# An attention and mixture-of-experts block: heads in the inner loop, chunks of queries in the outer one

## The chip, the cores and the metric

The kernel runs on one core of a Trainium2 chip. The core has five engines that work side by side, each through its own list of instructions in order: PE (TensorE, matrix products; its weight loads are listed as PEld), DVE (VectorE), ACT (ScalarE), POOL (GpSimd) and SP (SyncE), which here only issues transfers. The metric is the time of one execution on the device in microseconds. All data are float32.

## The reference

There are 2048 tokens of 256 numbers. The block computes causal attention with 16 heads of 16 numbers, adds it to the input and normalises; then a mixture of experts, adds that and normalises again.

```
q = x @ Wq;  c = x @ Wkv_down;  k = c @ Wk_up;  v = c @ Wv_up      # c has 64 columns
q, k: rotary position on 12 of each head's 16 numbers
x1 = layernorm(x + softmax(mask(q @ k.T / 4)) @ v)
p = softmax(x1 @ gate.T)                      # 16 experts, the two best of each token
y = sum over the two: p_e * (silu(x1 @ w1_e.T) * (x1 @ w3_e.T)) @ w2_e.T    # 176 inner
z = the same form with one shared expert of 352 inner
out = layernorm(x1 + y + z)
```

## The kernel before

**Tiles.** The tokens are cut into four chunks c of 512 (CH), the heads into four groups g of four (G). The four heads of a group lie on 32 partitions each[...]. `prologue(c)` transposes a chunk of x into `xT[c]` and multiplies it down to `ckv[c]`. `project_k(g, c)` makes the rotated keys of a group and a chunk: two products on PE, two DVE instructions into the one buffer `rot` (pool wk1), and a POOL addition into `ks[g, c]`. `project_q` makes `qs[g, c]` (PE, then DVE), `project_v` makes `vs[g, c]` (PE, ACT, and a POOL fill of a column of ones). `double(g)` is three small POOL copies that complete a group's weights once they are loaded.

**Two passes of products.** A softmax needs the largest score of each query. The kernel first computes all scores for the maxima alone (`Maxima`, the tiles m: PE products, reduced on DVE into pm by `tensor_reduce`, or with the mask by `tensor_tensor_reduce` where keys and queries are of one chunk). When all maxima of (g, c) are there, `negated` gathers them into nm (DVE), and `shift` transposes nm on PE (pn) and adds it to the queries on DVE: the result is `qa[g, c]`. A second pass computes the scores transposed with qa (`Weighted`, tiles s), ACT takes exponentials (p), POOL masks the diagonal squares, and PE multiplies by the values (av). ACT copies av to `more` and POOL adds it to avs; in a step without m, DVE adds it directly. `finish(g, c)` transposes avs (po), divides by the sum and adds the result to x in `xr[c]`; after the last group it also takes means and variances.

**Steps.** The order is written out by hand in the list `steps`. Each step is a pair of an m unit (g, c, t, kc) and an s unit (g, c, kb), either of which may be missing. A unit is four products of up to 512 columns; it is "whole" where keys and queries are of different chunks, and "diagonal" where they are of one, with 512, 384, 256 and 128 columns in turn. In a pair the two halves interleave: two heads of s beside two of m, then the reverse. The av products of a step are issued after the products of the next step. The list before runs group by group: group 0 through chunks 0 to 3, then each other group from chunk 3 down to 0, and the last group through chunks 3, 0, 1, 2. `put(step, what)` hangs everything else on step numbers: projections, prologues, shift, finish, and the router. All eight PSUM banks are one rotating pool for these tiles (`bank`). PE keeps the order of the program; the other engines' lists are put in order when the kernel is built.

**Router and experts.** For a chunk with all groups finished, `normed` normalises on DVE, `turned` transposes to `x1T[c]`, `choose` computes logits (lg) and picks two experts, `settle` counts places (pc) and `scatter` sends each row by eight indirect transfers of POOL to its expert's room in the DRAM buffer xg, which SP filled with blank rows before. The chunk LAST is routed after attention. Then `table`, `load_block`, `turn`, `hidden`, `turn_hidden` and `output` run 47 blocks of 128 rows, each through the expert that its rows belong to, and POOL scatters the results to yg. `shared_hidden` and `shared_out` compute the shared expert; `fetch` and `combine` add up, normalise and write.

**Memory and loads.** Keys and values of the running groups live in the pool kv, eight buffers of k and six of v. The experts' weights w13 (44 KB on each partition) are loaded early by SP, after x, the rotary tables cs and cq and the projections' weights, and before the blank fill of xg. The rotary table for keys of chunk 3, cs3, has a tile of its own; the other three become the shared expert's weights later.

Of the kernel before, what the change touches and what calls it, by code (L numbers as in the profile page):

```python
# [17 lines left out]
P = 128  # L18
# [19 lines left out]
WARM = 3  # L38
LAST = 2
DEPTH = 6  # L40
# [6 lines left out]
def block_kernel(  # L47
# [39 lines left out]

    cs = [const.tile([P, 2, CH], F32, tag=f"cs{c}", name=f"cs{c}") for c in range(3)]

# [39 lines left out]
    for c in range(NCH):  # L129
        nc.gpsimd.tensor_copy(  # L130
            xr[c][:, :, E : E + 1], number[:, 4 * c : 4 * c + 4].unsqueeze(2)
        )

    blank = hot.rearrange("p j t n -> p (j t n)")[:, :ROW]
    nc.gpsimd.memset(blank, 0.0)
    nc.gpsimd.tensor_copy(blank[:, E : E + 1], number[:, TT:])

# [147 lines left out]
    with ExitStack() as att:  # L285
        ap1 = att.enter_context(tc.tile_pool(name="ap1", bufs=1))
        kv = att.enter_context(tc.tile_pool(name="kv", bufs=8))
        wk1 = att.enter_context(tc.tile_pool(name="wk1", bufs=1))
# [14 lines left out]
        )  # L303
        cs.append(ap1.tile([P, 2, CH], F32, tag="cs3", name="cs3"))
        cq = [ap1.tile([P, CH], F32, tag=f"cq{c}", name=f"cq{c}") for c in range(NCH)]
# [46 lines left out]
        load_rope(0, False, nc.sync)  # L352
        load_x(1)
        load_rope(0, True, nc.scalar)
        double(0)
        for a in range(2):
            nc.sync.dma_start(out=wvs[a * LAT : (a + 1) * LAT], in_=wv[:LAT])
        load_rope(1, False, nc.sync)
        load_rope(1, True, nc.sync)
        load_x(2)  # L360
        load_rope(2, False, nc.sync)
        load_rope(2, True, nc.sync)
        load_x(3)
        load_rope(3, False, nc.sync)
        load_rope(3, True, nc.sync)
        for g in range(1, G):
            load_weights(g, nc.sync)
        nc.sync.dma_start(out=gw, in_=gate.rearrange("(k p) n -> p k n", p=P))
        for j, w in ((0, w1), (1, w3)):
            for k in range(2):  # L370
                nc.sync.dma_start(
                    out=w13[:, k, :, j * INTER : (j + 1) * INTER],
                    in_=w[k * P : (k + 1) * P, :NF].rearrange("p (n f) -> p n f", f=INTER),
                )

        def load_shared():
# [4 lines left out]
            for i, (o, m) in enumerate(SCH):  # L381
                nc.sync.dma_start(out=sw2[:m, i, :], in_=w2[NF + o : NF + o + m, :])


        for e in range(NEXP):
# [28 lines left out]
        def project_k(g, c):  # L414
            tmp = wk1.tile([P, 2, CH], F32, tag="rot", name=f"rot{g}_{c}")
            pk = [bank(f"pk{g}_{c}_{a}") for a in range(2)]
            for a in range(2):
                r = slice(a * LAT, (a + 1) * LAT)
                matmul(
                    pk[a], lhsT=wks[g][r], rhs=ckv[c][r], start=True, stop=True  # L420
                )
            nc.vector.scalar_tensor_tensor(  # L422
                tmp[:, 0, :], pk[0], unit, cs[c][:, 0, :], ALU.add, ALU.mult
            )
            nc.vector.tensor_tensor(tmp[:, 1, :], pk[1], cs[c][:, 1, :], ALU.mult)  # L425
            ks[g, c] = kv.tile([P, CH], F32, tag="k", name=f"k{g}_{c}")
            nc.gpsimd.tensor_tensor(ks[g, c], tmp[:, 0, :], tmp[:, 1, :], ALU.add)  # L427
# [11 lines left out]
        def project_v(g, c):  # L439

            pv = [bank(f"pv{g}_{c}_{a}") for a in range(2)]
            for b in range(4):
# [6 lines left out]
                )  # L449
            v = kv.tile([P, CH], F32, tag="v", bufs=6, name=f"v{g}_{c}")  # L450
            for a in range(2):
# [47 lines left out]
        def shift(g, c, nm):  # L499

            pn = bank(f"pn{g}_{c}")
            for t in range(4):
                transpose(
                    pn[:, t * P : (t + 1) * P], nm[:, t].rearrange("p h d -> p (h d)"), ident
                )
            qa[g, c] = wk3.tile([P, CH], F32, tag="qa", name=f"qa{g}_{c}")
            nc.vector.tensor_tensor(qa[g, c], qs[g, c], pn, ALU.add)
# [83 lines left out]
        def diagonal_m(g, c):  # L591
            return [(g, c, t, c) for t in reversed(range(4))]
# [9 lines left out]

        def spread(whole, diagonal, n):

            out, whole = [], list(whole)
            for d in diagonal:
                out += whole[:n] + [d]
                whole = whole[n:]
            return out + whole

        def add(ms, ss, pattern=None):

            ms, ss = list(ms), list(ss)
            pattern = pattern or "1" * max(len(ms), len(ss))
            for p in pattern:
                steps.append((ms.pop(0) if ms else None, ss.pop(0) if p == "1" else None))
            assert not ms and not ss, (ms, ss)


        add(diagonal_m(0, 0), [], "0000")  # L620
        add(whole_m(0, 1), [], "0000")
        add(diagonal_m(0, 1), diagonal_s(0, 0))
        add(whole_m(0, 2), whole_s(0, 1, [0]), "00011011")
        add(diagonal_m(0, 2), diagonal_s(0, 1))
        add(whole_m(0, 3), whole_s(0, 2, [0, 1]), "000111101111")
        add(diagonal_m(0, 3), diagonal_s(0, 2))
        m = whole_m(1, 3)
        add(m[:4], [], "0000")
        add(
            spread(m[4:], diagonal_m(1, 3), 2) + diagonal_m(1, 2),  # L630
            spread(whole_s(0, 3, [0, 1, 2]), diagonal_s(0, 3), 2),
        )
        for g in range(1, G):
            add(
                spread(whole_m(g, 2), diagonal_m(g, 1), 2) + whole_m(g, 1),
                spread(whole_s(g, 3, [2, 1, 0]), diagonal_s(g, 3), 2),
            )
            if g + 1 == G:

                add(diagonal_m(g, 2), diagonal_s(g, 0))  # L640
                add([], diagonal_s(g, 1) + whole_s(g, 1, [0]))
                add([], whole_s(g, 2, [1, 0]) + diagonal_s(g, 2))
            else:
                m = whole_m(g + 1, 3)
                add(
                    spread(m[:8], diagonal_m(g, 0), 2),
                    spread(whole_s(g, 2, [1, 0]), diagonal_s(g, 2), 2),
                )
                add(
                    spread(m[8:], diagonal_m(g + 1, 3), 1),  # L650
                    spread(whole_s(g, 1, [0]), diagonal_s(g, 1), 1),
                )
                add(diagonal_m(g + 1, 0 if g + 2 == G else 2), diagonal_s(g, 0))

# [14 lines left out]

        for step, what, c in (  # L670
            (1, project_k, 1), (1, project_q, 1), (3, prologue, 2), (4, project_v, 0),
            (6, project_k, 2), (7, prologue, 3), (9, project_v, 1), (9, project_q, 2),
            (14, project_k, 3), (17, project_q, 3), (19, project_v, 2), (32, project_v, 3),
        ):
            if what is prologue:
                put(step, what, c)
            else:
                put(step, what, 0, c)
        for g in range(1, G):
            i = m_first[g, NCH - 1]  # L680
            put(5, double, g)
            for c in range(NCH):
                put(i + (-14, -11, -8, -6)[c], project_k, g, c)
                put(min(i + (32, 24, 13, -3)[c], m_first[g, c] - 3), project_q, g, c)
                put(i + (24, 22, 17, 13)[c], project_v, g, c)
        for (g, c), i in m_last.items():
            def late(i=i, g=g, c=c):
                nm = negated(g, c)
                put(i + 2, shift, g, c, nm)
            put(i, late)  # L690
            assert i + 3 <= s_first[g, c]
        for (g, c), i in s_last.items():
            put(i + (4 if g + 1 < G else 2), finish, g, c)
            if g == G - 1:
                put(i + 2, normed, c)
                if c != LAST:
                    put(i + 6, turned, c, bank)
                    put(i + 7, lambda c=c: chosen.update({c: choose(c, bank)}))
                    put(i + 11, lambda c=c: settle(c, bank, chosen[c]))
                    for t in range(4):  # L700
                        put(i + 12, scatter, c, t)

        put(s_first[G - 1, 3], load_shared)

# [4 lines left out]
        prologue(0)  # L709
        project_k(0, 0)  # L710
        project_q(0, 0)
        prologue(1)
        prior = None
# [258 lines left out]

    shared_hidden(3, 0)
    shared_hidden(3, 1)
    turned(LAST, spare)
    shared_hidden(3, 2)
    both = choose(LAST, spare)
    shared_out(3)
    shared_hidden(0, 0)
    settle(LAST, spare, both)  # L980
# [5 lines left out]
    key = keys(end)  # L986
    shared_hidden(0, 1)
    shared_hidden(0, 2)
    shared_out(0)
    shared_hidden(1, 0)  # L990
    turn(0)
# [10 lines left out]
    output(NBLK - 1, key)  # L1002
    shared_hidden(1, 1)
    shared_hidden(1, 2)
    shared_out(1)
    shared(LAST)
    fetched = {}
    for n, h in enumerate((6, 7, 0, 1, 2, 3, 4, 5)):
        fetched[h], load = fetch(h)
        if n == 0:  # L1010
            wait_for(back, load)
# [68 lines left out]
```

## Time and profile before

| | us |
|---|---|
| runs, median of three (lowest, highest) | 824.31 (823.65, 827.38) |
| the profiled execution, its own time | 821.03 |
| its span, first to last instruction | 819.3 |
| PE busy (share of the span) | 790.6 (96%) |
| DVE busy | 552.0 (67%) |
| ACT busy | 452.9 (55%) |
| POOL busy | 328.0 (40%) |
| first m product | 19.6 |
| last finish of attention begins | 597.65 |
| first product of an expert | 642.2 |

The span is what the profile's times count in; the execution's own time lies 1.7 us above it. The granted clock of PE is 0.988 of full speed on average. DMA moves 72.6 MB, most of it between 60 and 180 us, when the experts' weights and the blank rows go. A busy PE means only that a product is under way: products overlap, and their ends are modelled.

### The profile page before, as it was taken

Reading aid. Unit: us, or ns where it says so; the run is one execution under the profiler, and the core shown is the slowest. Engines: PE = TensorE matmul, PEld = TensorE weight load, DVE = VectorE, ACT = ScalarE, POOL = GpSimd, SP = SyncE. Lnnn points to the kernel's source line nnn. Section 1 sums busy time; section 2 is a strip of 40 time slices with the busy share of each in tenths; the row PEclk is TensorE's granted clock in tenths of the full one; section 3 lists DMA queues with packets and bytes.
Section 4 is the critical chain, followed back from the end, with each engine's and each line's share of the span. In section 5 each row is a group of like instructions: output and inputs, shape, how many; then the busy total and the mean of one; then the engine's idle time right before and its main releaser. Section 6 shows DMA issues by size and latency. Waiting matters only on the chain. (4 is left out here: it accounts for less than half of the span.)

```text
span 819.3 us, 15191 instructions
## 1 busy us (share of the span) xinstructions
PE 790.6 (96%) x5146; PEld 371.8 (45%) x5146; DVE 552.0 (67%) x1503; ACT 452.9 (55%) x1014; POOL 328.0 (40%) x562
## 2 busy tenths in 40 slices
PE   7999999999999999999999999999999899999994
PEld 3444433534333344534344444443356466666652
DVE  2769888986777887787887777887466233333266
ACT  1143556387776886676786668756531233333346
POOL 2042535344454554455354546433553133333300
PEclk9999999999999999999999999999899999999998
DMA  5479999960000000010000000001152322222062
GB/s 145 130 190 334 325 331 325 318 191 2 1 1 2 1 1 2 1 36 18 2 1 1 2 1 1 2 1 53 52 161 78 98 84 86 83 79 76 16 206 102
DMA packets 68339, 72.56 MB, mean 89 GB/s; under 512 B 5056, under 2 KB 62499, under 8 KB 68262
## 3 DMA queue, kind: packets, MB, share of 16 engines
q1 hardware_dynamic: 63006, 62.43, 26.3%
q0 software_dynamic: 3792, 8.43, 2.9%
q10 hardware_dynamic: 1464, 0.72, 0.4%
q8 instruction: 42, 0.69, 0.3%
q14 instruction: 35, 0.29, 0.1%
HBM read 27.10 MB, written 46.43 MB: 90 GB/s over the span
## 5 line engine op out<-in xcount | busy, mean ns | idle before, releaser
L534 ACT ACTIVATE p<-s 128x512 f32<-128x512 f32 (+3 forms) x640 | 292.7, 540 | 131.6 <-PE m L139 77.5
L139 PE MATMUL m<-k,q 32*128 32x512 f32 (+3 forms) x1280 | 303.3, 564 | 0.8 <-DVE rot L422 0.5
L139 PE MATMUL s<-qa,k 32*128 32x512 f32 (+3 forms) x1280 | 280.4, 558 | 3.3 <-DVE avs L562 2.3
L489 DVE TENSOR_REDUCE pm<-m 128x1 f32<-128x512 f32 x384 | 237.5, 681 | 44.0 <-PE m L139 43.6
L566 POOL TENSOR_TENSOR avs<-avs,more 128x512 f32<-128x512 f32 (+3 forms) x125 | 136.8, 1094 | 166.4 <-ACT more L565 162.8
L139 PEld LDWEIGHTS s<-qa,k 32*128 32x128 f32 x1280 | 107.3, 184 | 120.3 <-ACT p L534 67.4
L139 PE MATMUL av<-p,v 128*32 128x512 f32 (+3 forms) x1280 | 156.6, 546 | 0.9 <-ACT p L534 0.4
L139 PEld LDWEIGHTS m<-k,q 32*128 32x128 f32 x1280 | 122.8, 183 | 44.4 <-issue 12.0
L484 DVE CUSTOM_DVE_ANT_0 m<-m,qmask 128x512 f32<-128x512 f32 (+3 forms) x256 | 118.2, 521 | 28.8 <-PE m L139 25.8
L565 ACT COPY more<-av 128x512 f32<-128x512 f32 (+3 forms) x125 | 65.6, 525 | 38.3 <-PE av L139 31.4
L928 POOL DMA_INDIRECT yg<-yb,to x47 | 46.3, 985 | 99.1 <-DVE to L922 51.0
L538 POOL TENSOR_SCALAR_AFFINE_SELECT p<-p 128x128 f32<-128x128 f32 x256 | 70.6, 297 | 38.2 <-ACT p L534 36.4
L139 PEld LDWEIGHTS av<-p,v 128*32 128x32 f32 x1280 | 27.3, 108 | 104.5 <-ACT p L534 53.6
L139 PE MATMUL ph<-w,xbT 128*128 x188 | 68.8, 490 | 2.3 <-DVE xbT L881 1.7
L900 DVE TENSOR_TENSOR rh<-ru,ph 128x176 f32<-128x176 f32 x47 | 15.9, 337 | 61.9 <-ACT ru L898 61.9
L898 ACT ACTIVATE ru<-ph 128x176 f32<-128x176 f32 x47 | 14.9, 318 | 66.9 <-PE ph L139 65.6
L139 PE MATMUL py<-w2r,hT 88*128 x188 | 48.5, 380 | 0.5 <-ACT hT L907 0.5
L139 PE MATMUL h<-xT,cs 128*128 128x512 f32 (+1 forms) x96 | 43.3, 597 | 2.4 <-ACT u L791 1.4
L277 POOL DMA_INDIRECT xg<-xr,slot x32 | 31.1, 972 | 32.6 <-issue 21.3
L139 PEld LDWEIGHTS ph<-w,xbT 128*128 128x128 f32 x188 | 32.4, 191 | 23.2 <-issue 13.4
L139 PEld LDWEIGHTS py<-w2r,hT 88*128 88x128 f32 x188 | 35.5, 189 | 13.3 <-ACT hT L907 1.1
L427 POOL TENSOR_TENSOR k<-rot 128x512 f32<-128x512 f32 x16 | 20.3, 1268 | 42.6 <-DVE rot L425 42.6
(146 smaller groups left out, 649.0 us busy)
## 6 DMA issues: line engine op xcount, KB each, us to landing
xg<-hot SPq DMA_DIRECT2D x16, 2064.0 KB
xb<-xg SPq DMA_DIRECT2D x47, 129.0 KB
w<-in_w_dram SPq DMA_DIRECT2D x4, 1408.0 KB
got<-yg SPq DMA_DIRECT2D x8, 512.0 KB
w2r<-in_w_dram SPq DMA_DIRECT2D x2, 1408.0 KB
xr<-in_x_dram SPq DMA_DIRECT2D x4, 512.0 KB
out_dram<-o SPq DMA_DIRECT2D x8, 256.0 KB
cs<-in_rope_dram SPq DMA_DIRECT2D x16, 80.0 KB
```

The costliest lines, as they stand in the source:

```text
L139: tc.keep_in_program_order(op(*args, **kw))
L277: put = nc.gpsimd.indirect_dma_start(out=xg[:, :], out_offset=bass.IndirectOffsetOnAxis(ap=slot[:, j, i : i + 1], axis=0), in_=xr[c][:, t, ...
L427: nc.gpsimd.tensor_tensor(ks[g, c], tmp[:, 0, :], tmp[:, 1, :], ALU.add)
L484: nc.vector.tensor_tensor_reduce(out=ps[:, :n], in0=ps[:, :n], in1=qmask[:, CH - n :], scale=1.0, scalar=3.0 * NEG, op0=ALU.add, op1=ALU.m ...
L489: nc.vector.tensor_reduce(to, ps, AX.X, ALU.max)
L534: nc.scalar.activation(pr[:, n0:], ps[:, n0:], AF.Exp, scale=SCALE)
L538: nc.gpsimd.affine_select(out=diag, in_=diag, pattern=[[1, P]], base=0, channel_multiplier=-1, compare_op=ALU.is_ge, fill=0.0,)
L565: nc.scalar.copy(more[:, n0:], pv[:, n0:])
L566: nc.gpsimd.tensor_tensor(to, to, more[:, n0:], ALU.add)
L898: nc.scalar.activation(u, ph[:, :INTER], AF.Silu)
L900: nc.vector.tensor_tensor(us[b], u, ph[:, INTER:], ALU.mult)
L928: nc.gpsimd.indirect_dma_start(out=yg[:, :], out_offset=bass.IndirectOffsetOnAxis(ap=to[:, 0:1], axis=0), in_=yb, in_offset=None, bounds_c ...
```

## The change

The loops change places. Attention runs chunk by chunk, and all four groups within each chunk, from chunk 0 to chunk 3: job i is (g, c) with g running fastest. While job i's s units run, the whole m units of job i+1 and the diagonal ones of job i+2 run beside them; projections of k and q are made three jobs ahead. So keys and values of every group must stay to the end of attention: the pool kv goes, and the 32 tiles lie in `places`, 22 of them inside w13 and ten in tiles of their own. The weights of the experts are loaded in two halves by `load_experts` when groups 1 and 2 of the last chunk are done. All groups' projection weights are loaded at the start, three groups are projected before the first step, and the rotary tables of chunk 3 use the tile of chunk 0. Chunks 0, 1 and 2 are routed between the steps of the following chunk; LAST is 3. qa has two buffers instead of three, and the blank rows have a tile of their own. In the last stage chunks take each other's places.

```diff
-LAST = 2
+LAST = 3
...
-    cs = [const.tile([P, 2, CH], F32, tag=f"cs{c}", name=f"cs{c}") for c in range(3)]
+    cs = [const.tile([P, 2, CH], F32, tag=f"cs{c}", name=f"cs{c}") for c in range(NCH - 1)]
+    cs.append(cs[0])
...
-        kv = att.enter_context(tc.tile_pool(name="kv", bufs=8))
...
+        room13 = w13.rearrange("p k n f -> p (k n f)")
+        places = [room13[:, i * CH : (i + 1) * CH] for i in range(2 * NEXP * 2 * INTER // CH)]
+        places += [
+            ap1.tile([P, CH], F32, tag=f"kv{i}", name=f"kv{i}")
+            for i in range(2 * G * NCH - len(places))
+        ]
...
         load_weights(0, nc.scalar)
         load_rope(0, False, nc.sync)
-        load_x(1)
         load_rope(0, True, nc.scalar)
-        double(0)
+        load_weights(1, nc.sync)
+        load_weights(2, nc.sync)
         for a in range(2):
             nc.sync.dma_start(out=wvs[a * LAT : (a + 1) * LAT], in_=wv[:LAT])
+        load_weights(3, nc.sync)
+        for g in range(G):
+            double(g)
+        load_x(1)
         load_rope(1, False, nc.sync)
         load_rope(1, True, nc.sync)
         load_x(2)
+        load_x(3)
         load_rope(2, False, nc.sync)
         load_rope(2, True, nc.sync)
-        load_x(3)
-        load_rope(3, False, nc.sync)
         load_rope(3, True, nc.sync)
-        for g in range(1, G):
-            load_weights(g, nc.sync)
...
-            ks[g, c] = kv.tile([P, CH], F32, tag="k", name=f"k{g}_{c}")
+            ks[g, c] = places[2 * NCH * g + c]
...
-            v = kv.tile([P, CH], F32, tag="v", bufs=6, name=f"v{g}_{c}")
+            v = places[2 * NCH * g + NCH + c]
...
-            qa[g, c] = wk3.tile([P, CH], F32, tag="qa", name=f"qa{g}_{c}")
+            qa[g, c] = wk3.tile([P, CH], F32, tag="qa", bufs=2, name=f"qa{g}_{c}")
...
+        jobs = [(g, c) for c in range(NCH) for g in range(G)]
+        ahead = {0: (0, 0, 0, 0), 1: (2, 4, 4, 4), 2: (3, 6, 8, 8), 3: (4, 8, 12, 12)}
+        add(diagonal_m(*jobs[0]), [])
+        add(diagonal_m(*jobs[1]), [])
+        for i, (g, c) in enumerate(jobs):
+            ss = whole_s(g, c, reversed(range(c)))
+            ms = whole_m(*jobs[i + 1]) if i + 1 < len(jobs) else []
+            whole = [(ms[j], ss[j]) if j < len(ss) else (ms[j], None) for j in range(len(ms))]
+            whole = whole or [(None, u) for u in ss]
+            more = len(whole) - len(ss)
...
+            ds = diagonal_s(g, c)
+            dm = diagonal_m(*jobs[i + 2]) if i + 2 < len(jobs) else [None] * 4
+            diagonal = list(zip(dm, ds))
+            if c:
+                diagonal = diagonal[2:] + diagonal[1::-1]
...
+            if i + 3 < len(jobs):
+                put(d384, project_k, *jobs[i + 3])
+                put(d128, project_q, *jobs[i + 3])
+            if i + 1 < len(jobs):
+                put(d256, project_v, *jobs[i + 1])
+            if g == 0 and c + 1 < NCH:
+                put(d384, prologue, c + 1)
+        put(s_first[1, 0], load_rope, NCH - 1, False, nc.sync)
+        for k in range(2):
+            put(s_last[k + 1, NCH - 1], load_experts, k)
...
-                put(i + 2, shift, g, c, nm)
+                put(max(i + 2, s_first[g, c] - 3), shift, g, c, nm)
...
             if g == G - 1:
-                put(i + 2, normed, c)
-                if c != LAST:
-                    put(i + 6, turned, c, bank)
-                    put(i + 7, lambda c=c: chosen.update({c: choose(c, bank)}))
-                    put(i + 11, lambda c=c: settle(c, bank, chosen[c]))
+                put(i + (2 if last else 5), normed, c)
+                if not last:
+                    i += (40, 20, 8)[c]
+                    put(i, turned, c, bank)
+                    put(i + 2, lambda c=c: chosen.update({c: choose(c, bank)}))
+                    put(i + 6, lambda c=c: settle(c, bank, chosen[c]))
                     for t in range(4):
-                        put(i + 12, scatter, c, t)
+                        put(i + 8 + t, scatter, c, t)
...
         prologue(0)
-        project_k(0, 0)
-        project_q(0, 0)
-        prologue(1)
+        for n, job in enumerate(jobs[:3]):
+            project_k(*job)
+            project_q(*job)
+        project_v(*jobs[0])
```

The order that results, by step: 0 to 7 m alone (the diagonals of jobs 0 and 1), 8 to 27 chunk 0, 28 to 63 chunk 1, 64 to 115 chunk 2, 116 to 179 chunk 3. Steps 20, 22, 24, 25, 52, 54, 57, 60, 100, 102, 104 and 107 hold a whole m alone; 152, 157, 162 and 163 hold a diagonal s alone, and from 164 on all hold s alone.

## The prediction

> **What bounds the kernel now.** I read the stages first, as windows of busy time by engine: start, early attention, steady attention, the end of attention, the stretch up to the experts, the experts, the combination. Columns: busy time of PE, PEld, DVE, ACT, POOL (instructions), granted clock, DMA share, GB/s.
>
> ```profile
> 0.00:60.00 60.00, 53.54 (x254) 24.17 (x258) 34.04 (x97) 14.53 (x33) 15.46 (x56) 0.97 0.55 151
> 60.00:156.00 96.00, 95.83 (x652) 39.34 (x648) 81.49 (x176) 48.19 (x106) 39.29 (x68) 1.00 1.10 327
> 156.00:534.00 378.00, 376.35 (x3037) 158.07 (x3034) 298.64 (x743) 273.40 (x602) 183.76 (x320) 1.00 0.07 21
> 534.00:600.00 66.00, 62.08 (x430) 25.36 (x431) 44.58 (x180) 38.19 (x86) 28.39 (x57) 0.95 0.11 36
> 642.00:780.00 138.00, 136.63 (x564) 87.46 (x565) 43.69 (x138) 47.93 (x141) 45.71 (x47) 0.99 0.24 72
> ```
>
> The reader is to see that PE is busy everywhere, which says little: early attention holds 6.8 matmuls per us (652 in 96 us), steady attention 8.0. In the early stretch DVE is busy 85%, so PE stretches while it waits for banks; in the steady stretch DVE is busy 79%, ACT 72%, and PE's own pace counts. The pace is read from the timeline of one paired step (start, duration, engine, tile):
>
> ```profile
> 403.94 0.70 PE L139 MATMUL s<-qa,k 32*128 32x512 f32 x2
> 405.87 1.06 PE L139 MATMUL av<-p,v 128*32 128x512 f32 x8
> 406.86 0.70 PE L139 MATMUL s<-qa,k 32*128 32x512 f32 x2
> 408.02 2.07 ACT L534 ACTIVATE p<-s 128x512 f32<-128x512 f32 x4 [0.32 <-PE m L139]
> 408.10 2.48 DVE L489 TENSOR_REDUCE pm<-m 128x1 f32<-128x512 f32 x4 [0.22 <-PE m L139]
> ```
>
> From 403.94 to 405.87 run the eight products of m and s (1.93 us), then av (0.99): 2.92 us a step on PE, against 2.48 on DVE and 2.66 on ACT (2.07 and a 0.59 copy). A step with m alone is the reverse: PE 1.14, DVE 2.48. Last, the waits in 534 to 600 us (total us, times, longest):
>
> ```profile
> ACT p L534 <- PE s L139: 23.6, 17, 3.4
> DVE avs L562 <- PE av L139: 6.9, 7, 3.1
> DVE avs L562 <- PE s L139: 6.5, 2, 5.0
> ```
>
> No engine is full there: the routers of chunks 3, 0 and 1 lie between the last twenty steps, and PE, DVE and ACT wait for each other in turn.
>
> [...] The clock of 0.83 in 560 to 580 us fits: there products of s take 2.0 us for 1.1. [...] eight products of 32 rows take 1.93 us together, 0.59 to 0.70 each. A pair is thus as long as its longer half.
>
> **The method.** I price PE's program step by step and compare with the starts of steps in the trace (first product of s or m of each step). Prices from the timeline: paired 512 columns 1.93 + 0.99; 384: 1.67 + 0.78; 256: 1.46 + 0.57; 128: 1.25 + 0.37 (the four of a diagonal 9.02); m alone 1.14 (diagonal set 3.3); s alone 1.14 + 0.99 (diagonal set 6.0); project_k 1.13, project_q 1.98, project_v 1.15, shift and finish 0.6 each, a prologue 3.1, a router 3.9 (transposes 1.1, logits 1.94, counts 0.82). Before: 84 pairs with a whole s 245, 14 paired diagonal sets 126, m alone 21, s alone 37, projections with shifts and finishes 16 x 5.46 = 87, prologues 12, routers 12: 540 us. Attention ends at 598.3 (start of the last finish plus 0.6), so 58 us are lost, and by sections: before step 12 (59.7 us, 39.8 priced) 20; steps 12 to 49 (116.3 measured, 98.9 priced) 17, these hold twelve m-alone steps; steps 50 to 149 (327, 321) 6; step 150 to the end (93.9, 79) 15.
>
> **The change by parts.**
>
> *Products.* Both orders have 180 steps: 140 paired, 20 m alone, 20 s alone. Before, four diagonal m are paired with whole s and sixteen whole m are alone; after, eight diagonal and twelve whole are alone and all pairs match: 0.5 to 1 us less. Projections, routers, exponentials, reductions are as many as before. Priced: 539.5.
>
> *Start.* Three heads' groups are projected before the first m. SP issues weights 1 to 3 and wv before x1. The last sines of group 2 are issued at about 16.4 us (x0 and the rope loads end at 11.9 in the trace; 2 x 2.2 us of issues follow) and land some 2.5 later. By the built order POOL does the doublings of groups 1 and 2 ahead of the first k (end 19.8), and rot has one buffer, so k0 (1.27), rot1 (1.35), k1 (1.27), rot2 (1.35), q2 (0.7) run one after the other: DVE's first reduction starts at 25.8 instead of 20.78. Two diagonal sets on DVE (7.2 each and one shift) follow; PE runs two steps ahead through eight banks, so step 8 starts at 38.7. Priced work done by then is 20.8: 17.9 lost, and 2.5 in the first prologue behind exponentials. 20.4 against 20: +0.5. The later loads (x1 at 20, ropes to 44, the zero fill of xg 44 to 152 after 101 us of issues as now, the fourth rope behind it on SP) are due later still: the fourth rope at step 83, about 300 us. They cost nothing, covered by steps 8 to 83.
>
> *m alone.* Twelve whole ones, now laid between pairs in three jobs: DVE 20.3, 30.2, 40.2 us against PE 19.0, 30.7, 42.4. With the 7 to 10% that DVE-tight sections show now (12 to 24: 35.7 measured over 30.7): 10 lost for 17: -7.
>
> *Middle.* 116 other steps at the 0.06 us a step of steps 50 to 149 lose 7; two prologues wait for ACT, 1 us each; three routers put some 7 us of small DVE work each into stretches where DVE has 83 to 93% of PE's load: 4 in all; the dense first jobs 1.5. Together 14.5 against 6: +8.5. The scatters (24 x 1.27 us on POOL) hide under POOL's 50% idle time.
>
> *Borders of jobs.* Now shift precedes the first s by many steps. After, at eight borders (into chunk 1, chunk 2's first three, all of chunk 3) shift is issued after the job's last step and the next instruction on PE is s with that qa. Queued on PE: everything. The qa addition takes 0.68 and starts 0.07 after the transposes in the trace (404.07): 0.8 us each, 6.4, and 0.6 for DVE's backlog: +7. No trace shows this wait; its bounds are 0 (PE has av and a projection to do meanwhile) and 3.4 (DVE a whole step behind, 2.6 more).
>
> *End.* Twelve whole and four diagonal s alone with no router between: PE 2.13 a step, ACT 2.07. 2 lost for 15: -13. This includes the half clock (6.8 us at half, 3.4 lost).
>
> *Experts' weights.* 5.8 MB now go at about 507 and 552 us, behind nothing on SP; the zero fill moved at 320 to 345 GB/s, so 9 us for each half. Due at about 637: hidden by at least 75 us. K and V need no buffers to come free any more; none waited before. From the end of attention to the end the order is the same with chunks renamed: 221 us kept, in the experts' stage by 47 scatters on POOL and their landings.
>
> Sum: -0.5 + 0.5 - 7 + 8.5 + 7 - 13 = **-4.5 us**. The profiled execution took 821.03 (span 819.3), so it becomes 816.5; the median of the runs is 824.31, 3.3 above, so I predict **819.8**. A measurement of this kernel can tell about 0.5%, 4.1 us, from no change.
>
> **Rivals.**
> 1. *The borders decide: slower.* Without the borders the sum is -11.5 us, so from 1.4 us at each of the eight on the change loses. With DVE behind by 1.8 us, two thirds of a step's four reductions, each costs 2.6 and all 21: +9.5, 834. For it: DVE is at 93% of PE in the first job of chunk 3, and settle's work falls two steps before two borders. Against it: DVE drains while PE does av and projections.
> 2. *All bubbles go.* Borders covered by av and projections (-7), m alone costs only the greater of DVE and PE (-3): 809. For it: steps 50 to 149 lose 2% only, all extras included.
> 3. *No gain because the end is not freed:* the end's 15 us are lost again, as ACT waits for PE step by step (2.13 against 2.07), while the rest holds: 824 with some of the borders hidden. Against it: steps 167 and 171 took 2.07.
>
> **How the numbers follow.** Forecast 0.45, of it half beyond 4.1 us faster (0.24), 0.17 within, 0.04 slower; rival 2 0.22; rival 1 0.25; rival 3 0.08, nearly all within. Faster 0.46, same 0.24, slower 0.30. The likeliest case's own range is 813 to 827. Bounds: borders 0 to 24, m alone 3 to 17, routers and prologues 0 to 14, end 0 to 9, start -3 to +5; all together -20 and more to +26, and 806 to 836 leaves 2 in 10 out.
>
> **What would show it.** Right: first reduction near 26 us; step 8 near 39; last finish near 594; PE waiting for qa about eight times at 0.8 us; clock 1.00 in the last 40 us of attention; the stretch from there to the end within 1 us of 221. Wrong: a border above 1.4 us, early attention at under 7 matmuls per us in chunks 1 to 3, or a first product of an expert that waits for w13.

## The result, and the profile after

The changed kernel took **872.09 us** (median of four runs, 869.63 to 874.27) against 824.88 us for the kernel before (median of four, 823.65 to 827.38): 1.057 times as long, 95% interval 1.053 to 1.061. The profiled execution has a span of 871.8 us and a mean granted clock of PE of 0.952 (before: 819.3 and 0.988). Of these 52.5 us, 47.4 had been lost when the last step of attention began (595.2 us before, 642.6 now). The forecast was 819.8 us with a range of 806 to 836: it was wrong, in size and in sign.

The stages first. The first three windows are those of the prediction; the fourth reaches to the end of attention, which is later now, and the fifth holds the experts. Columns: busy time of PE, PEld, DVE, ACT and POOL with instructions, granted clock, DMA share, GB/s.

```profile
0.00:60.00 60.00, 53.93 (x262) 29.29 (x262) 34.62 (x121) 12.38 (x30) 19.11 (x62) 0.86 0.65 179
60.00:156.00 96.00, 91.09 (x660) 41.78 (x654) 72.65 (x218) 48.09 (x120) 40.74 (x95) 0.93 1.10 302
156.00:534.00 378.00, 360.09 (x2556) 149.60 (x2556) 286.37 (x723) 220.74 (x481) 170.31 (x273) 0.95 0.05 16
534.00:645.00 111.00, 108.64 (x889) 37.84 (x882) 69.36 (x130) 91.80 (x198) 37.88 (x70) 1.00 0.19 53
693.00:832.00 139.00, 137.47 (x563) 88.05 (x564) 42.87 (x138) 47.87 (x141) 45.31 (x47) 0.98 0.25 71
```

PE is still "busy" 95% of the third window, but it started 2556 products in the 378 us where the kernel before started 3037 (as the profile counts them: it has 24 records for the twelve products of a paired step), and its clock, which was 1.00 there, is 0.95. The loss is in the middle of attention. The end (fourth window) and the experts run at their pace.

A paired step that nothing disturbs costs what it did. Start, duration, engine, tile:

```profile
149.63 0.70 PE L136 MATMUL s<-qa,w 32*128 32x512 f32 x2
...
150.79 2.06 ACT L543 ACTIVATE p<-s 128x512 f32<-128x512 f32 x4 [2.19 <-PE m L136]
150.87 2.48 DVE L498 TENSOR_REDUCE pm<-m 128x1 f32<-128x512 f32 x4 [0.44 <-PE m L136]
...
151.56 1.06 PE L136 MATMUL av<-p,w 128*32 128x512 f32 x8
152.56 0.70 PE L136 MATMUL s<-qa,w 32*128 32x512 f32 x2
```

From 149.63 to 152.56 is 2.93 us, against the 2.92 of before. At the end of attention (534 to 645 us) ACT's waits for s, 23.6 us before, are down to 6.5:

```profile
ACT p L543 <- PE m L136: 10.3, 20, 2.1
ACT p L543 <- PE s L136: 6.5, 10, 1.6
...
DVE avs L571 <- PE av L136: 26.7, 16, 3.6
```

So the time went in single steps between. I priced each step as the prediction does and subtracted the price from the measured time. What is left is the loss, in us:

| steps | what lies there beside the pairs | lost |
|---|---|---|
| 28 to 35 | normalisation of chunk 0, a prologue | 10.0 |
| 64 to 75 | normalisation of chunk 1, choice and scatters of chunk 0, a prologue | 18.1 |
| 76 to 87 | choice of chunk 1 | 9.0 |
| 88 to 99 | scatters of chunk 1 | 7.5 |
| 116 to 131 | all of the router of chunk 2 | 19.0 |
| 20 to 27, 52 to 63, 100 to 115 | the m units alone | 13.3 |
| the other 71 between steps 12 and 179 | | 7.9 |

The first five rows are 64 us, and they hold the three routers. The waits of PE between 60 and 534 us say on which engines (total, times, longest):

```profile
PE s L136 <- DVE pm L498: 7.0, 6, 3.1
PE s L136 <- DVE qa L516: 4.9, 5, 1.2
PE av L136 <- issue: 3.4, 3, 1.7
PE av L136 <- POOL p L547: 3.1, 2, 2.4
```

The kernel before had next to none there; its longest was this:

```profile
PE s L139 <- DVE mv L585: 0.6, 1, 0.6
```

The four lines are 18 us only. In all PE was idle for 24.9 us between 60 us and the last s step, and for 4.5 us before. The rest is mostly the clock: between 100 and 500 us the trace has eight windows at half clock, 54.5 us together; the kernel before has none between 33 and 571 us. An estimate that counts half of their length as lost gives 27 us, where the one window of before, at 571 us, cost 3. So idle time (20 us more) and clock (24 more) make up 44 of the 47 us. Three of the windows, in the columns of above:

```profile
258.60:272.30 13.70, 13.70 (x54) 6.01 (x54) 9.05 (x29) 3.75 (x8) 1.50 (x2) 0.50 0.01 1
340.50:350.70 10.20, 9.78 (x26) 3.75 (x26) 4.63 (x16) 1.70 (x4) 1.88 (x5) 0.50 0.00 0
490.70:497.50 6.80, 6.20 (x22) 2.07 (x26) 3.62 (x6) 1.38 (x3) 0.82 (x1) 0.50 0.00 0
```

The timeline shows how it comes about. The first place is DVE at step 69, in the normalisation of chunk 1:

```profile
255.35 0.66 DVE L498 TENSOR_REDUCE pm<-m 128x1 f32<-128x512 f32 x1
255.93 0.16 DVE L151 TENSOR_SCALAR nv_ln<-mv 128x4 f32<-128x4 f32 x1
...
257.71 0.16 DVE L157 SCALAR_TENSOR_TENSOR na_ln<-nb_ln 128x4 f32<-128x4 f32 x1
257.79 0.68 DVE L498 TENSOR_REDUCE pm<-m 128x1 f32<-128x512 f32 x1
...
258.53 1.19 PE L136 MATMUL s<-qa,w 32*128 32x512 f32 x1 [0.48 <-DVE pm L498]
...
259.26 1.37 DVE L169 TENSOR_SCALAR xr<-xr,mv,nb_ln 128x256 f32<-128x256 f32 x4
...
260.55 2.47 DVE L498 TENSOR_REDUCE pm<-m 128x1 f32<-128x512 f32 x4
...
263.27 3.60 PE L136 MATMUL lg<-gw,xT 128*128 128x16 f32 x16
```

Between the reductions at 255.35 and 260.55 stand the dependent instructions of `inverse_root` and four of 0.34 us; only two of the reductions get between them. PE must wait for the banks that the reductions set free. No single wait is longer than 0.5 us, but few products start, and from 258.6 on each takes twice its time: lg 3.60 us for the 1.94 of the price list. The second place is POOL, at step 75:

```profile
292.89 0.97 POOL L274 DMA_INDIRECT xg<-xr,slot  x1 [0.31 <-ACT p L543]
293.88 0.30 POOL L547 TENSOR_SCALAR_AFFINE_SELECT p<-p 128x128 f32<-128x128 f32 x1
294.24 0.83 PE L136 MATMUL av<-p,w 128*32 128x384 f32 x2 [1.67 <-issue]
294.36 0.99 POOL L274 DMA_INDIRECT xg<-xr,slot  x1 [0.18 <-issue]
295.36 0.30 POOL L547 TENSOR_SCALAR_AFFINE_SELECT p<-p 128x128 f32<-128x128 f32 x1
295.72 1.11 PE L136 MATMUL av<-p,w 128*32 128x384 f32 x2 [0.65 <-POOL p L547]
...
296.77 3.35 PE L136 MATMUL pq<-xT,wqs 128*128 128x512 f32 x4
```

Each mask of a diagonal p stands behind a scatter, av waits for the mask, and pq then takes 3.35 us for 1.98.

### The profile page after: what moved, and what is told of

It reads as the page before. It is cut to its first block, busy times and chain, and to the rows that moved or that the text cites. A ratio compares the mean times of both kernels' runs of the same rounds, so it can differ in the third digit from the quotient of the medians.

```text
span 871.8 us, 15219 instructions
## 1 busy us (share of the span) xinstructions
PE 821.2 (94%) x5146; PEld 385.2 (44%) x5146; DVE 558.2 (64%) x1504; ACT 452.4 (52%) x1013; POOL 324.2 (37%) x561
## 5 line engine op out<-in xcount | busy, mean ns | idle before, releaser
L136 PE MATMUL s<-qa,w 32*128 32x512 f32 (+2 forms) x960 | 232.0, 574 | 14.1 <-DVE pm L498 7.0
L136 PE MATMUL m<-w,q 32*128 32x512 f32 (+3 forms) x960 | 236.2, 601 | 1.2 <-DVE rot L431 0.4
L575 POOL TENSOR_TENSOR avs<-avs,more 128x512 f32<-128x512 f32 (+3 forms) x124 | 133.3, 1075 | 210.0 <-ACT more L574 209.9
L136 PEld LDWEIGHTS s<-qa,w 32*128 32x128 f32 x960 | 89.2, 191 | 100.4 <-ACT p L543 55.2
L136 PEld LDWEIGHTS m<-w,q 32*128 32x128 f32 x960 | 98.4, 196 | 38.0 <-issue 9.9
L136 PE MATMUL av<-p,w 128*32 128x512 f32 (+3 forms) x864 | 110.0, 566 | 4.1 <-issue 3.4
L136 PE MATMUL m<-kv,q 32*128 32x512 f32 (+3 forms) x320 | 81.3, 574 | 2.1 <-DVE pm L493 1.4
L136 PE MATMUL s<-qa,kv 32*128 32x512 f32 (+3 forms) x320 | 63.9, 562 | 0.9 <-DVE qa L516 0.9
L136 PE MATMUL av<-p,kv 128*32 128x512 f32 (+3 forms) x416 | 53.6, 541 | 2.7 <-POOL p L547 2.7
L136 PEld LDWEIGHTS av<-p,w 128*32 128x32 f32 x864 | 17.8, 109 | 77.5 <-ACT p L543 37.7
L136 PEld LDWEIGHTS ph<-w,xbT 128*128 128x128 f32 x188 | 33.0, 195 | 23.9 <-issue 14.2
```

The costliest lines, as they stand in the source:

```text
L136: tc.keep_in_program_order(op(*args, **kw))
L575: nc.gpsimd.tensor_tensor(to, to, more[:, n0:], ALU.add)
```

## The experiments

The theories, by the names that the expectations use. **QUEUES**: a row of small DVE instructions or of scatters stands in order ahead of the reductions or the masks, PE waits for it, and its clock halves afterwards. **ORDER**: the loss belongs to the order chunk by chunk itself, to its borders, prologues and m units alone. **BUSY**: the routers cost their busy time, wherever they stand. **CLOCK**: the clock falls by itself. **HIDDEN**: idle time of DVE and POOL takes the work, as the prediction had it. Ratios are to the kernel before on the same chip, with 95% intervals; its median varied from 818.0 to 825.6 us over the chips that were used. Stages are compared by trace, and a trace too carries a difference between chips: the last s step of one and the same kernel (p3_both_pinned, p3_again) began at 598.7 us on one chip and at 601.4 on another.

### Four edits that the planner partly undid

The planner is the part of the build that puts the lists of DVE, ACT, POOL and SP in order.

**r1_routers_end** moves the routers in the program to the last job:

```diff
-                    i += (40, 20, 8)[c]
-                    put(i, turned, c, bank)
+                    i = s_first[jobs[-1]] + 4 * c
+                    put(i - 2, normed, c)
+                    put(i, turned, c, bank)
```

> The changed kernel with the routers of chunks 0, 1 and 2 (normalise, transpose, logits, choice, places, scatters) moved out of the middle of attention into the steps of the last job, 164 to 179, as the kernel before has them; the means and variances stay in the step of finish. QUEUES (the routers' small DVE instructions and their scatters on POOL stand in order ahead of the reductions and of the masks, PE waits for these, and its clock halves afterwards): steps 28 to 132 lose the routers' share, some 50 us, and the end gives 12 to 20 back: 825 to 840 us. ORDER (what was lost lies in the chunk-by-chunk order itself: waits for qa at every border, m units alone, prologues): 860 us or more, with long steps still at 33, 70, 87 and 127.

Measured: 854.17 us, ratio 1.037 (1.032 to 1.041). Steps 76 to 99 lost 2.0 instead of 16.5, steps 64 to 75 9.3 instead of 18.1, steps 116 to 131 8.1 instead of 19.0; the last job lost 9.9 instead of 2.2. But steps 33, 69 and 122 stayed long (14.2, 10.1, 7.9): in the trace the normalisations of chunks 0 to 2 still run at 129.9, 255.4 and 430.8 us. Only PE keeps the order of the program; the planner had taken DVE's free instructions forward again. The time lies between the two expectations and meets neither.

**r2_scatter_late** moves the scatters alone, one to each step of `whole_steps` (groups 1 and 2 of the last chunk, whole s):

```diff
-                    for t in range(4):
-                        put(i + 8 + t, scatter, c, t)
+                    for n in range(8):
+                        put(whole_steps[8 * c + n], scatter, c, n // 2, (n % 2,))
```

> The changed kernel, only the 24 scatters moved: one in each paired step of groups 1 and 2 of the last chunk instead of eight in four steps after each choice. QUEUES: the waits of av and exponentials behind eight scatters at steps 71-75, 92-95 and 127-131 go, with the slow clock after them: about 854 us, 18 less than the changed kernel; the stalls at 33, 69, 87 and 122 stay. ORDER: 872 us, no difference.

Measured: 868.82 us, 1.056 (1.051 to 1.061). In the trace all 24 scatters stand in the same steps as in the changed kernel: 74 and 75, 90 to 92, 130 and 131. The move did not reach the chip, so the run decides nothing.

**r3_dve_spread** makes generators of the router's functions and takes two instructions from them after each step (the counts pc are copied out of their PSUM bank first, so that the bank can go on):

```diff
+                    def onward(step, parts, c):
+                        for _ in range(PACE):
+                            if next(parts, parts) is parts:
+                                done(c, step)
+                                return
+                        put(step + 1, onward, step + 1, parts, c)
```

> The changed kernel, the scatters in groups of eight as they were, but the DVE instructions of each router (means and variances, inverse root, normalise, choice, places) handed out two in each step, from six steps after the last unit of the chunk, so that none stands in a row of more than two ahead of a reduction. QUEUES: about 836 us, 36 less; steps 33, 69, 70, 87 and 122 fall to their prices, the ones after the scatters stay. ORDER: above 860 us. CLOCK (PE's clock falls by itself and not after a wait): the half-clock windows stay as many as in the changed kernel.

Measured: 880.68 us, 1.069 (1.065 to 1.073): slower. The planner had drawn the choice together into one row in the middle of step 49, which took 10.7 us, with m reductions only behind it:

```profile
196.72 0.22 DVE L237 TENSOR_REDUCE gates<-rest 128x4 f32<-128x64 f32 x1
...
198.00 0.22 DVE L259 TENSOR_TENSOR both<-hot 128x64 f32<-128x64 f32 x1
198.15 1.28 DVE L544 TENSOR_REDUCE pm<-m 128x1 f32<-128x512 f32 x2
...
198.88 0.79 PE L137 MATMUL s<-qa,w 32*128 32x128 f32 x2 [3.17 <-DVE pm L544]
```

So it tests a row at another place, and there too PE waits 3.17 us. **r4_both** adds the edit of r2 to it:

> Both edits at once: two DVE instructions of a router in each step, and one scatter in each paired step of groups 1 and 2 of the last chunk. QUEUES: about 818 us, 54 less than the changed kernel, with half-clock windows only at the start and in the last stage. ORDER: above 855 us. CLOCK: windows of half clock remain in the middle though the waits are gone.

Measured: 880.94 us, 1.069 (1.065 to 1.073), as r3: its scatters too had come forward, the eight of a chunk in two or three steps.

### The same edits with the order held

Now each router instruction is tied behind the instruction that the program has before it on its engine. The tie orders the issue and waits for nothing:

```diff
+            return lambda *args, **kw: tc.keep_in_program_order(getattr(nc.vector, op)(*args, **kw))
...
-            put = nc.gpsimd.indirect_dma_start(
+            put = tc.keep_in_program_order(nc.gpsimd.indirect_dma_start(
```

> As r1_routers_end, but means and variances and the normalisation of chunks 0, 1 and 2 are tied behind the DVE instruction that the program has before them, in steps 161 to 170, so that the planner can't bring them forward to steps 33, 69 and 122, where r1_routers_end still had them. QUEUES: steps 33, 69 and 122 fall by 4 to 5 us each with the slow clock that follows, the end takes some 3 us more: about 843 us, against 854. ORDER (steps 33, 69 and 122 are long because of the prologue and the border): within 3 us of r1_routers_end.

Measured for **p1_end_pinned**: 845.46 us, 1.024 (1.021 to 1.027). Step 33 fell from 14.2 to 6.5 us, step 69 from 10.1 to under 4.6, and steps 28 to 35, 64 to 75 and 116 to 131 lost 2.2, 2.1 and 2.1. The prologue and the border in steps 28 to 35 thus cost 2 of the 10; the row of the normalisation cost 8. But the routers in a row at the end make the last job lose 20.7, 11 more than in r1 where 3 were expected; the steps before it gained more than expected as well, so the time came close to the 843 in part by luck.

> As r3_dve_spread, but each DVE instruction of a router tied behind the DVE instruction before it in the program, so that they stay two to a step; in r3_dve_spread the planner drew them together again, 12 in a row at step 49. QUEUES: no row of small instructions is longer than two, steps 33, 69, 70, 87, 122 and, of r3_dve_spread, 49, 59, 85 lose their waits: 840 to 850 us, what is left being the scatters. BUSY (DVE has no room left beside the reductions, 4 of 0.68 in a step of 2.92, wherever the instructions stand): above 865 us.

> The changed kernel with only the scatters moved and tied, one in each paired step of groups 1 and 2 of the last chunk; in r2_scatter_late the planner brought them back to where they were. QUEUES: the waits of av and of the exponentials at steps 71 to 75, 92 and 127 to 131 go: 855 to 862 us, 10 to 17 less than the changed kernel. ORDER: within 3 us of 872.

> As p2_dve_pinned, and the scatters one in each paired step of groups 1 and 2 of the last chunk, tied in the same way on POOL. QUEUES: about 827 us, 45 less than the changed kernel; the half-clock windows between 100 and 500 us go. BUSY: above 855 us. CLOCK (PE's clock falls by itself): the windows stay where they were.

| kernel | us | ratio (95%) | last s step begins | half clock, 100 to 500 us |
|---|---|---|---|---|
| changed | 872.09 | 1.057 (1.053 to 1.061) | 642.6 | 54.5 |
| p4_scatter_pinned: scatters one a step | 854.67 | 1.034 (1.031 to 1.037) | 624.4 | 37.5 |
| p2_dve_pinned: DVE two a step | 844.33 | 1.022 (1.020 to 1.024) | 613.2 | 20.5 |
| p3_both_pinned | 831.09 | 1.007 (1.005 to 1.008) | 598.7 | 6.8 |

The scatters alone give 18 us of attention back, the DVE work alone 29, both 44 of the 47 by which attention had grown; on the chip of p3_again it is 41. The work is all still there; p3 even has three copies more. (In p3 and p4 two of the 24 scatters still came forward, singly.) The scatters were both spread out and moved to another stage, so these runs don't tell which of the two mattered. The waits of PE on rows are gone; of those between 60 and 560 us the largest in p3 are these:

```profile
PE s L137 <- DVE qa L572: 6.7, 7, 1.2
PE av L137 <- POOL p L603: 0.9, 1, 0.9
```

Here are the windows of p3 for steps 28 to 35, 64 to 75, 76 to 87, 88 to 99 and 116 to 131, in the same columns:

```profile
111.00:141.00 30.00, 29.75 (x232) 13.39 (x228) 22.07 (x60) 19.52 (x45) 12.67 (x26) 0.96 1.09 327
236.00:280.00 44.00, 42.56 (x324) 17.90 (x324) 36.50 (x88) 30.29 (x65) 20.45 (x33) 1.00 0.04 13
280.00:324.00 44.00, 42.92 (x340) 19.24 (x344) 36.43 (x92) 28.85 (x63) 19.04 (x31) 1.00 0.00 1
324.00:364.00 40.00, 39.98 (x314) 16.78 (x307) 36.01 (x87) 28.69 (x62) 18.62 (x31) 1.00 0.01 2
411.00:465.00 54.00, 52.87 (x412) 21.35 (x416) 47.24 (x111) 39.25 (x82) 24.80 (x37) 1.00 0.03 8
```

The last four run at full clock with DVE busy for 83 to 90% of the time. This refutes CLOCK for seven of the eight windows: they went when the rows went. The eighth, of 6.8 us, begins at 108.4 us in the changed kernel and at 106.3 in p3; no row of a router stands ahead of it, so it belongs to the order (more on it at the end). ORDER is refuted for 44 of the 47 us (41 by p3_again). BUSY fails as well, since the work is all there. Of the 44 us, half of the 47.7 us of half clock that vanished makes 24 by estimate, and PE's idle time fell by 14, from 24.9 to 10.6; the last 6 are in neither.

### The disputed cost by itself, in the kernel before

Into the middle of the attention of the kernel before I put work that nothing needs.

```diff
+        for n in (60, 80, 100, 120):
+            put(n, row)          # b1: 12 of 128x4, 4 of 128x256 on DVE; b2: 8 of 128x512 on POOL
...
+        for n in range(64):      # b3: the instructions of b1, one after each step
+            put(60 + n, one, 4 if n % 16 < 12 else E)
```

> The kernel before, with four rows of DVE instructions that nothing needs, after steps 60, 80, 100 and 120, in the middle of its attention: twelve of 128x4 and four of 128x256, the shapes of one normalisation, each feeding the next, some 4 us in a row. The disputed cost by itself, in a kernel whose attention has no half-clock window from 34 to 570 us. QUEUES: each row holds up the reductions behind it, PE waits for its banks, and the clock halves: 4 to 8 us for each row, 840 to 856 us in all, with new half-clock windows that begin within 10 us of a row. HIDDEN (the prediction's premise: DVE's idle third takes it): 825 to 829 us, no new window.

> The kernel before, with four rows of eight POOL additions of 128x512 that nothing needs, at the same four steps: 10 us in a row, as long as eight scatters. QUEUES: the additions to avs and the masks stand behind the row, ACT's copy finds no buffer, the exponentials behind it and then av and the banks wait: 3 to 6 us for each row, 837 to 850 us. HIDDEN (the prediction's premise: POOL's 60 per cent of idle time takes it): 825 to 829 us.

> The kernel before with the same 64 unneeded DVE instructions as b1_dve_rows, but one after each of the steps 60 to 123 instead of sixteen after each of four. The work is the same, only the rows are gone. QUEUES: hardly dearer than the kernel before, at most 5 us, and no new half-clock window. BUSY (the instructions cost their own time wherever they stand): 16 us more, the sum of the four rows' lengths.

Measured: **b1_dve_rows** 847.51 us, 1.036 (1.034 to 1.038). By the trace the four rows cost 6.5, 7.6, 4.2 and 7.5 us, 25.8 from step 60 to step 130, and half-clock windows of 6.8, 6.8, 3.4 and 6.8 us begin with them. One of the rows:

```profile
216.34 3.36 DVE L711 TENSOR_SCALAR heap<-heap 128x4 f32<-128x4 f32 x12
...
219.73 1.41 DVE L715 TENSOR_SCALAR heap<-heap 128x256 f32<-128x256 f32 x4
...
221.05 2.48 DVE L489 TENSOR_REDUCE pm<-m 128x1 f32<-128x512 f32 x4
221.79 1.22 PE L139 MATMUL s<-qa,k 32*128 32x512 f32 x1 [2.13 <-DVE pm L489]
...
226.10 1.94 PE L139 MATMUL av<-p,v 128*32 128x512 f32 x8
```

The row is 4.7 us long, PE waits 2.13, and then av, which by the trace waits for nothing more, takes 1.94 us for 1.06. **b2_pool_rows** took 836.24 us, 1.022 (1.020 to 1.025): rows of eight additions of 1.04 us cost 2.1, 6.9, 1.2 and 6.9 us. In the two dear ones the masks of a diagonal unit stand singly between the additions:

```profile
293.10 4.38 POOL L711 TENSOR_TENSOR heap<-heap 128x512 f32<-128x512 f32 x4
297.44 0.29 POOL L538 TENSOR_SCALAR_AFFINE_SELECT p<-p 128x128 f32<-128x128 f32 x1
...
297.79 2.74 PE L139 MATMUL av<-p,v 128*32 128x384 f32 x4 [3.77 <-POOL p L538]
```

In the other two the eight ran in one go of 8.9 us. These are the longest rows of all and the cheapest: by the trace they began 6 to 7 us ahead of the exponentials whose masks stood behind them (218.66 against 225.03, 358.31 against 365.65), and av waited 1.3 and 0.4 us. So the length alone isn't the price; by these four rows it is how long after the need the row ends. The expectation, 3 to 6 us for each row, was met by none of the four, and the whole came out just under its range. **b3_dve_single** took 826.82 us, 1.010 (1.006 to 1.014): between steps 60 and 130 the work of b1 costs 7.5 us instead of 25.8, and no half-clock window lies between 57 and 555 us. HIDDEN falls by b1, BUSY by b3 (16 us expected). QUEUES expected at most 5 here; single instructions are cheap, not free. For POOL there is no such run with the additions one to a step.

### What is left: borders and the tail

p6_border issues `shift` one step earlier, p5_border_tail also orders the last diagonal set as the kernel before does:

```diff
-                put(max(i + 2, s_first[g, c] - 3), shift, g, c, nm)
+                put(max(i + 1, s_first[g, c] - 3), shift, g, c, nm)
...
-            if c:
+            if c and i + 1 < len(jobs):
                 diagonal = diagonal[2:] + diagonal[1::-1]
```

> As p3_both_pinned, with the queries' shift issued one step after the last m unit of its group and chunk instead of two, so that qa has a step's time until the first s product. If the 7.6 us for which s products waited for qa at the borders are a real cost: 823 to 826 us. If only the wait changes its place (pn then waits for nm, or the reductions wait for the addition of qa): 830 us or more.

> As p6_border, and the last job ends with its diagonal unit of 128 columns, as the kernel before does, instead of the one of 512, whose exponentials, masks and av stand alone at the end: 2.5 to 3 us less than p6_border, so 820 to 823 us, level with the kernel before. If the end is set by something else: equal to p6_border.

Measured: **p6_border** 827.12 us, 1.012 (1.010 to 1.014), and **p5_border_tail** 824.53 us, 1.008 (1.007 to 1.010). Both miss their expectations (823 to 826 and 820 to 823) by 1.1 and 1.5 us. The ratio of p6 is higher than that of p3, but that chip ran the kernel before in 818.0 us and the chip of p3 in 825.6. So all three went to one chip:

> p3_both_pinned again, on one chip with p6_border and p5_border_tail, whose chip ran the kernel before 7 us faster than that of p3_both_pinned: the ratio to the kernel before stays between 1.005 and 1.0085.

> The earlier shift beside p3_both_pinned on one chip. If the waits for qa at the borders are a real cost: 3 to 5 us below p3_again. If the wait only changed its place: level with it.

> The earlier shift and the narrow diagonal unit at the end, on the same chip: 2.5 to 3 us below p6_again, and within 0.5 per cent of the kernel before. If the end is set by something else: level with p6_again.

Measured: **p3_again** 833.14 us (831.03 to 834.03), **p6_again** 827.26 (826.60 to 828.97), **p5_again** 825.69 (824.06 to 826.22), the kernel before 819.25; ratios 1.016 (1.014 to 1.019), 1.011 (1.008 to 1.013) and 1.008 (1.005 to 1.010). The expectation for p3_again failed: its ratio follows the chip. The earlier shift gives 5.9 us, more than the 3 to 5 expected: the wait it removes was this one of p3_again, and in p6_again no s waits for qa.

```profile
PE s L137 <- DVE qa L572: 7.6, 8, 1.2
```

The tail gives 1.6 us more, less than the 2.5 to 3 expected, with no overlap of the runs. "Level with the kernel before" failed: p5_again is 0.8% slower, and no version here beats the kernel before. Where these last 6 us lie wasn't settled; the m units alone still lose 12 us in p5_again, but the kernel before had its own losses of that kind.

## Why the prediction was wrong

- **The prices held.** A paired step took 2.93 us for 2.92. That a pair is as long as its longer half shows in the trace before: where 512 columns of s stand beside 256 and 128 of m (201.64 and 204.44 us), the first av comes 1.81 us after the first s, against 1.93 for 512 beside 512.
- **The start was right.** First reduction 25.49 us (forecast 25.8), step 8 at 38.64 (38.7). That PE would be at half clock there from 26.5 to 43.5 us was not foreseen; it cost little, since p3, where it lasted from 27.8 to 34.7 us alone, begins step 8 at 37.9.
- **The m units alone** lost 13.3 us where 10 was given.
- **The borders** were right in kind and size: PE waited for qa seven times in the whole kernel, 6.9 us, longest 1.2 (forecast eight times, 6.4 and 0.6 for backlog). Rival 1 had the sign right for a cause that did not act: no border reached its 1.4 us. That p6_again gives back 5.9 us confirms the term.
- **The end was right.** The last job lost 2.2 us (forecast 2), and the clock was 1.00 from 498 us to the end of attention. The end had held the routers; the forecast counted that gain and charged too little for their new place.
- **The step that failed is "Middle", +8.5.** It gave the routers "4 in all" and the prologues "1 each", and let the 24 scatters "hide under POOL's 50% idle time". The five sections with the routers lost 64 us. With the other steps, and without the last job and the waits for qa, the middle lost some 62 where 14.5 were given; that is 47 of the 57 us by which the profiled execution, 873.7 us, missed its forecast of 816.5. Three things were wrong in it. The DVE work of a router was put at 7 us; summed in the trace, with means, variances and transposed copies, it is some 14. The work was set as a volume against idle time, though it comes as rows of up to 5 us in an in-order queue, ahead of reductions that eight banks wait for; b1 and b3 show the same work at 25.8 and 7.5 us. And the scatters were costed at nothing with POOL's average as cover, though the masks of diagonal units stand in the same queue: p4 gives 18 us for them.
- **The half clock was seen and not carried over.** The prediction read the half clock at 560 to 580 us, where the routers of before stand, and took its 3.4 us off the end. That the same routers would bring it along was left out: seven windows, 47.7 us long, some 24 lost. PE had started 2 to 13 products in the 3.4 us ahead of these seven, and no single wait was longer than 3.1 us.
- **After attention** 221 us were kept in the forecast, and within 1 us of it was named as a sign of being right; from the last po (648.1) to the end it is 223.7, 2 more than before (597.65 to 819.3). Why wasn't settled. The last po itself came 5.5 us after the last s step began, before it 2.5. No product of an expert waited for w13: the first waits for xbT, 1.7 us, as before.
- **The signs.** Of the three signs of being wrong one came true: chunks 1 to 3 ran at under 7 products per us, 6.8 from 156 to 534 us.
- **Two sums.** Rival 3 doesn't make 824: without the gain of the end the sum is +8.5 us, or +1.5 with every border hidden, so 826 to 833. And steps 50 to 149 took 328.3 us in the trace before, 1 more than the prediction has. Neither bears on the step that failed.

## What to carry to other kernels

Before moving small work to another stage, ask what stands behind it in its engine's queue, and price the row by how long PE must wait for what stands behind it, not by the engine's average idle time. A row of 4.7 us ahead of the reductions cost 4.2 to 7.6 us here, half clock included; one of 8.9 us that began well before its masks were needed cost 1.2 and 2.1. Spread such work over the steps one or two instructions at a time and hold it there, since a planner may draw it together again; look into the trace whether a moved instruction did move. A list of waits shows only part of a loss when the clock falls: compare the granted clock and the products started per us as well.

## What was not expected of the hardware

Short waits were enough for half clock. At full pace PE starts 24 products, as the profile counts them, in a step of 2.92 us, so by estimate 28 in 3.4 us, the length of the shortest window in the changed kernel's attention. In the 3.4 us ahead of seven of the half-clock windows that the changed kernel shows from 130 to 500 us it had started 2 to 13, though no single wait there was longer than 3.1 us; ahead of the four that follow the rows of b1, 6 to 8. The nine windows in the changed kernel's attention, in order of time, lasted 17.1, 6.8, 6.8, 13.7, 3.4, 10.2, 3.4, 3.4 and 6.8 us.

The eighth window, at 108.4 us, doesn't go with a small number of products. PE had started 26 of them in the 3.4 us before, without any idle time; they belong to diagonal units and are 128 or 256 columns wide. Whether their width brought the window was not shown.

Five waits between 60 and 534 us of the changed kernel were of 1.4 us and more (3.1, 1.7, 1.4, 2.4 and 1.9 us); each ended within 2 us of the beginning of a window. A short wait at a border, 0.9 to 1.2 us in otherwise full steps, brought no window in p3, whose one window from 100 to 500 us is that at 106.3. What decides stays open.
